# A graph layer pair on one core: two transposes given to the DMA engines, one compare given to VectorE, and a new written-out order

## The chip, the cores and the metric

The kernel runs on one core of one Trainium2 chip. A core has TensorE (PE in the profile, with PEld for its weight loads), VectorE (DVE), ScalarE (ACT), GpSimd (POOL) and SyncE (SP, which only issues DMAs here), and 16 DMA engines behind them. The metric is device microseconds of one execution. Of three timed runs of the kernel before, the median is 966.61 us (966.36 to 968.12).

## The reference

There are 128 graphs of 128 nodes with 64 features. With F = 64 and H = 192 the reference computes, for each graph b:

```
# layer 0
mask = adj > 0
h[j,k,:] = relu(x[j] @ W1a + (x[j] - x[k]) @ W1b + b1)         # 128 x 128 x 192
hm[j,:]  = sum over k of h[j,k,:] * mask[j,k]
x = layernorm(x + hm @ W2 + deg[j] * b2)
# layer 1
m   = relu(relu(x @ V1 + c1) @ V2 + c2)
msg = relu(adj @ m)
r, z, n = GRU gates of (msg, x)
x = layernorm(x + (1 - z) * n + z * x)
```

The sum over k runs only over the neighbours of j, and most nodes have few. So the kernel gathers the projected rows of the neighbours with matmuls against one-hot matrices, and does not form all 128 x 128 pairs.

## The kernel before

The 128 graphs are worked off in 32 groups of G = 4 graphs. For one group the work is a set of named parts, each a Python generator whose steps end at `yield`:

- `load`: three kinds of DMA on SP's queue (`adjT`, `xT` in two halves, `x`), lines 397, 403 and 405.
- preparation: `masks` (POOL, L415), `ranks` (a matmul with a triangular matrix gives the rank of every neighbour in its row; ACT copies it to `rankT`, L425), `degrees`, `counts`, `offsets` (first segment numbers, then `till`, four POOL compares of `iota` with a per-partition limit `off`, L466, then a matmul L469 that gives `own`, the owner of each extra segment), `turned` (four PE transposes of `rankT`, L487, and an ACT copy, L490), `owners` (four PE transposes of `own`, L495, and an ACT copy to fp32, L498), `places` (9 matmuls that need `rank` and `own`, L504 to L511), `pick0` and `pick1` (VectorE compares that make the one-hot matrices, L518, L532, L540), `values0` and `pieces` (the projections, split into three bf16 pieces).
- the gathers, the bulk: `seed0`/`seed1` (ACT writes a start value to a PSUM tile, L606), `gather0`/`gather1` (12 matmuls 64 x 192 each, L636, 24 such steps for a group), and their readers, `keep0`/`keep1` (ACT relu, L656) and `reduce`/`reduce1` (VectorE relu and add in one instruction, L666, 18 for a group). A PSUM tile is read before the next gather adds to it; there are three such tiles (pool `ps_g`).
- `base`, `together`, `joined` (ACT and POOL fold the sums), `sums0`/`sums2` (PE, L711, L718 and L723, for graphs 0, 1 and 2, 3; the second uses `ownT`).
- the tail of a group, made by `tail_parts`: `second` (L284, L288, layernorm), `turn`, `message1` to `message3`, `gates`, `update` (layernorm and the store, L743). For the last group `filler` adds matmuls without use between steps of this chain.

Small PSUM tiles of all these parts share a pool `ps_w` with two buffers.

The order is written out by hand. TIMETABLE gives each step of each part a number; group g adds g * PER to it (PER = 100000), FIRST replaces some numbers for group 0 and SETUP gives those of the constants. All steps are sorted by number and emitted in that order, and each engine then works through its own instructions in that order. So parts of four or so groups are interleaved, and the numbers set only the order and not a time. Every engine's queue, SP's too, is strictly in order: an instruction that waits holds all that stand behind it.

After the groups a branch for inputs with too many neighbours follows, which is not taken here; its test costs a small matmul and a register load at the end.

Of the kernel before, what the change touches and what calls it, by code (L numbers as in the profile page):

```python
# [8 lines left out]
F32 = mybir.dt.float32  # L9
BF16 = mybir.dt.bfloat16  # L10
I32 = mybir.dt.int32
AF = mybir.ActivationFunctionType
ALU = mybir.AluOpType
AX = mybir.AxisListType

N = 128
# [15 lines left out]
    "load": (-268618,), "masks": (-266066,), "ranks": (-232900, -232900), "degrees": (-257102, -254423),  # L32
    "turned": (-224742, -220574), "counts": (-234901,), "offsets": (-217678, -211964, -197704, -192380, -189932),
    "owners": (-35894, -35894), "places": (-179586, -177714),
    "pieces": (-221915, -212465, -212465, -212025, -212025, -210034, -207896, -206287, -204509, -201502, -201502),
    "others": (-93885, -63613), "values0": (-168677, -168312, -168312), "pick0": (-187243, -177588, -157318, -147219),
    "pick1": (-101562, -99096), "over0": (-86465, -86465), "over2": (-91716, -89070), "base0": (-71690,),
    "base1": (-115079,), "base2": (-74898,), "base3": (-66289,), "together0": (-90368, -86071, -54801),
    "sums0": (-16639, -16639, -6895), "joined0": (-42043,), "joined2": (-9054,),
    "together1": (-31159, -22707, -22707), "together2": (-54332, -29252, -26680), "sums2": (-10324, -7550, -6743),  # L40
    "together3": (-14410, -11697, -11388), "second": (1322, 1729, 6614, 12070, 12714, 14947), "turn": (17589, 19125),
    "message1": (22148, 22871), "message2": (24221, 25357), "message3": (34134, 47496),
    "gates": (52002, 52335, 59212, 59212, 60471, 61641),
    "update": (63484, 134926, 134926, 146356, 147450, 212137, 231447, 236648, 276814),
    "seed0": (-137838, -111380, -107532, -90909, -89996, -88760, -70167, -48540),
    "gather0": (-132826, -123102, -109699, -102053, -101463, -95122, -90696, -82750, -82750, -77811, -77618, -69952,
        -66122, -48012, -38905, -32104), "keep0": (-129922, -97944, -81962, -65602),
    "reduce": (-116740, -102949, -100299, -89511, -89215, -81357, -75312, -71801, -69013, -44762, -33692, -24596),
    "seed1": (-80653, -43141), "gather1": (-77673, -72671, -67801, -55447, -41338, -33923, -28108, -20295),
    "keep1": (-76545, -38998), "reduce1": (-70927, -59829, -52180, -31003, -23063, -16037),  # L50
# [3 lines left out]
SETUP = (-227883, -212853, -185033, -155144, -101231, 22249)  # L54
FIRST = {
    "load": (-236749, -176840), "masks": (-192323,), "ranks": (-160512, -153527), "degrees": (-172354, -159518),
    "turned": (-108605, -102394), "counts": (-146837,), "offsets": (-115482, -109556, -106790, -103472, -99536),
    "places": (-98687, -93949),
    "pieces": (-169807, -166786, -164278, -164278, -164278, -164278, -158634, -152826, -143767, -142875, -113691),
    "values0": (-148521, -139633, -130220), "pick0": (-141784, -133982, -133982, -103074), "pick1": (-92485, -74065),  # L60
    "over0": (-88306, -87641),
# [4 lines left out]
def adj_resnorm_kernel(  # L66
# [172 lines left out]

    def tail_parts(s, work, ps_w, n, store):


        name = s["name"]


        side = nc.vector if name == str(ng - 1) else nc.gpsimd

        def layernorm(y, tag, into):  # L250
            stats = work.tile([N, n, 6], F32, tag="st" + tag, name=f"stats{tag}_{name}")
# [640 lines left out]
```

## Time and profile before

| what | value |
|---|---|
| median of three runs | 966.61 us |
| the profiled execution's own time | 966.97 us |
| its span in the profile | 965.2 us |
| granted TensorE clock, mean | 0.980 |
| PE busy | 907.4 us, 94% |
| DVE busy | 827.3 us, 86% |
| ACT busy | 841.4 us, 87% |
| POOL busy | 840.7 us, 87% |
| distance between equal steps of two groups in the middle | 28.29 us |

Busy time of an engine is the union of its instructions; a group's row gives the number of instructions, their summed time and the mean of one, and then the idle time just before them with the engine that ended it. In a timeline row the first number is the start and the second the length, both in us.

### The profile page before, as it was taken

To read this page: it belongs to the slowest core of one execution; us is meant where nothing else is said; L and a number is where in the kernel's file an instruction comes from. 1 tells how busy PE (TensorE), PEld (TensorE's weight loads), DVE (VectorE), ACT (ScalarE), POOL (GpSimd) and SP (SyncE) were. 2 spreads that over 40 slices of the span, in tenths; PEclk is the share of its full clock that TensorE was granted. 3 is DMA by queue.
4 is the path that set the end of the run, shared out by engine and by line. 5 is a ranking of instruction groups with operands and counts; after the bars stand their busy time and mean duration, and the time that the engine had idled before them with its cause. 6 is when DMAs were issued, how large, how long until landed. Compare 5 with 4: busy or idle time off the path is not lost.

```text
span 965.2 us, 32667 instructions
## 1 busy us (share of the span) xinstructions
PE 907.4 (94%) x13333; PEld 723.1 (75%) x13335; DVE 827.3 (86%) x1586; ACT 841.4 (87%) x1762; POOL 840.7 (87%) x1233
## 2 busy tenths in 40 slices
PE   6888999999999999999999999999999999999984
PEld 3567777777877777878777787777778777777762
DVE  5687898888899888889988888988888898888962
ACT  3787899999999999999999999999999999999863
POOL 4576899999999999999999999999999999999774
PEclk6898999999999999999999999999999999999998
DMA  3000001111100111110001111011101001010000
GB/s 97 24 3 23 24 2 29 30 29 30 29 18 13 30 30 29 30 30 10 22 29 30 30 30 29 2 30 30 30 29 29 25 7 30 29 30 8 7 7 19
DMA packets 25565, 23.91 MB, mean 25 GB/s; under 512 B 4156, under 2 KB 21314, under 8 KB 25410
## 3 DMA queue, kind: packets, MB, share of 16 engines
q1 hardware_dynamic: 25410, 21.78, 7.9%
q8 instruction: 106, 1.74, 0.8%
q14 instruction: 49, 0.40, 0.1%
HBM read 17.57 MB, written 4.19 MB: 23 GB/s over the span
## 4 chain that ended last, share of the span: by engine, by line
PE 68%; ACT 14%; DVE 13%; issue 3%; POOL 1%; DMA 0%; SPq 0%; ACTq 0%; DVEq 0%; POOLq 0%
PE pv L636 32%; DVE acc L666 7%; ACT x L269 4%; PE ph L718 3%; PE pw L284 3%; PE pv L577 3%; ACT pv L606 3%; DVE pick L532 3%; ACT us L623 2%; PE pv L547 2%; PE pu L547 2%; PE ph L723 2%; PE ph L711 2%; PE pm L307 2%; PE pa L327 2%
## 5 line engine op out<-in xcount | busy, mean ns | idle before, releaser
L666 DVE SCALAR_TENSOR_TENSOR acc<-pv,acc 128x768 f32<-128x768 f32 x576 | 534.4, 952 | 102.6 <-PE pv L636 90.4
L636 PE MATMUL pv<-b,pick 64*128 64x192 bf16 x9216 | 465.9, 245 | 21.0 <-DVE acc L666 17.0
L636 PEld LDWEIGHTS <-pick 64*128 64x128 bf16 x9216 | 379.2, 95 | 92.9 <-issue 69.9
L606 ACT COPY pv<-u 128x768 f32<-128x768 f32 x256 | 206.3, 816 | 1.1 <-DVE acc L666 1.0
L656 ACT ACTIVATE acc<-pv 128x768 f32<-128x768 f32 x192 | 155.9, 812 | 17.1 <-PE pv L636 16.9
L686 POOL TENSOR_TENSOR acc<-acc 128x384 f32<-128x384 f32 x128 | 143.7, 1123 | 12.9 <-DVE acc L666 12.9
L466 POOL TENSOR_SCALAR till<-iota,off 128x128 bf16<-128x128 bf16 x128 | 100.3, 801 | 7.8 <-ACT off L458 7.8
L574 ACT CAST b<-pv 128x384 bf16<-128x384 f32 x192 | 83.0, 486 | 19.7 <-PE pv L547 10.5
L691 POOL TENSOR_TENSOR fs<-acc,nb 128x192 f32<-128x192 f32 x128 | 75.9, 593 | 21.6 <-ACT nb L678 14.1
L699 POOL TENSOR_TENSOR acc<-acc 128x384 f32<-128x384 f32 x64 | 77.8, 1216 | 7.3 <-DVE acc L666 7.2
L688 POOL TENSOR_TENSOR acc<-acc 128x192 f32<-128x192 f32 x128 | 77.9, 608 | 2.6
L518 DVE TENSOR_TENSOR pick<-rankT,ramp 128x2048 bf16<-128x2048 bf16 x64 | 77.2, 1208 | 0.7 <-POOL npad L448 0.7
L606 ACT COPY pv<-us 128x768 f32<-128x768 f32 x64 | 51.4, 803 | 26.4 <-DVE acc L666 26.4
L259 POOL TENSOR_SCALAR ve<-mv 128x4 f32<-128x4 f32 x64 | 39.5, 617 | 35.5 <-DVE mv L256 35.4
L263 POOL TENSOR_TENSOR rs<-ve,nhalf 128x4 f32<-128x4 f32 x64 | 66.8, 1043 | 0.0
L415 POOL TENSOR_SCALAR maskT<-adjT 128x512 bf16<-128x512 f32 x32 | 61.2, 1912 | 6.1 <-DMA adjT<-in_adjT_dram 6.0
L617 PE MATMUL pz<-u,own 128*128 128x192 f32 x256 | 57.7, 348 | 0.9 <-ACT own L474 0.9
L678 ACT ACTIVATE nb<-u,npad 128x192 f32<-128x192 f32 x128 | 58.5, 458 | 0.0
L532 DVE TENSOR_TENSOR pick<-pick 128x1024 bf16<-128x1024 bf16 x64 | 50.4, 787 | 0.0
L269 ACT ACTIVATE x<-y,nm,rs 128x64 f32<-128x64 f32 x128 | 45.9, 432 | 4.8 <-POOL nm L265 4.8
L269 ACT ACTIVATE o<-y,nm,rs 128x64 f32<-128x64 f32 x128 | 45.9, 446 | 2.2 <-POOL nm L265 2.2
L617 PEld LDWEIGHTS pz<-u,own 128*128 128x128 f32 x256 | 39.8, 189 | 9.3 <-ACT own L474 5.9
(148 smaller groups left out, 1635.6 us busy)
## 6 DMA issues: line engine op xcount, KB each, us to landing
adjT<-in_adjT_dram SPq DMA_DIRECT2D x32, 256.0 KB, 3.0
xT<-in_xT_dram SPq DMA_DIRECT2D x64, 64.0 KB, 2.7
x<-in_x_dram SPq DMA_DIRECT2D x32, 128.0 KB, 2.3
out_dram<-o SPq DMA_DIRECT2D x32, 128.0 KB, 1.7
wab<-in_w_dram SPq DMA_DIRECT2D x2, 96.0 KB, 2.9
bi<-in_b_ih_dram SPq DMA_DIRECT2D x1, 96.0 KB
bias<-in_b_hh_dram SPq DMA_DIRECT2D x1, 96.0 KB
wx<-in_w_hhT_dram SPq DMA_DIRECT2D x2, 48.0 KB, 2.7
```

The costliest lines, as they stand in the source:

```text
L269: nc.scalar.activation(s[into][:, i, :], y[:, i, :], AF.Identity, bias=nm[:, i : i + 1], scale=rs[:, i : i + 1])
L466: nc.gpsimd.tensor_scalar(s["till"][:, i, :], iota, off[:, i : i + 1], None, ALU.is_lt)
L532: nc.vector.tensor_tensor(v[:, q, 1], v[:, q, 1], v[:, q, 0], ALU.subtract)
L574: nc.scalar.copy(b[c][:, h::2, :], ps[h])
L606: nc.scalar.copy(v, src.to_broadcast(list(v.shape)))
L617: nc.tensor.matmul(p[:, i, :], s["own32"][:, i0 + i, :], s["u"][:, i0 + i, :], start=True, stop=True)
L636: nc.tensor.matmul(v[:, h, j, :], pick[ks], s[f"b{c}"][ks, gr, :], start=False, stop=c == 2, skip_group_check=True,)
L656: nc.scalar.activation(kept(s, t, i), view(s["pv", t, i, 0]), AF.Relu)
L666: nc.vector.scalar_tensor_tensor(out=a, in0=view(s["pv", t, i, k // CH if t == 0 else 0]), scalar=0.0, in1=a, op0=ALU.max, op1=ALU.add,)
L686: nc.gpsimd.tensor_tensor(f[:, 0], f[:, 0], f[:, 1], ALU.add)
L688: nc.gpsimd.tensor_tensor(f[:, 0, 0], f[:, 0, 0], f[:, 0, 1], ALU.add)
L699: nc.gpsimd.tensor_tensor(f[:, 0], f[:, 0], f[:, 1], ALU.add)
```

## The change

- `turned` and `owners` no longer use PE and PSUM. Each is one transposing DMA on SP's queue (128 x 512 bf16, four 128 x 128 blocks); `rank` comes straight from it, `ownT` is copied from a new bf16 tile `ownTh` (one buffer) to fp32 by ACT as before.
- `off` and its ACT copy are gone. `till` is one VectorE compare of 128 x 512 that reads the limits from PSUM, in place of four POOL compares of 128 x 128.
- The first group's `adjT` and `xT` are issued on ScalarE's queue.
- In the last group layer 1 is worked off as two pairs of graphs: parts with the ending `_a` for graphs 0 and 1, without fillers, and the usual parts for graphs 2 and 3. The dimensions that were 2 become n // 2.
- `sums` gets one more `yield`, between L718 and L723 of before.
- TIMETABLE, SETUP and FIRST are new throughout. Loads of a group stand 3.74 periods ahead of its base number where they stood 2.69 ahead, and `second` 1.02 periods ahead where it stood 0.01 behind; so the distance between the two is nearly the same.

```diff
 def loading(s):
-                nc.sync.dma_start(s["adjT"], adjT[:, gs, :])
+                q = nc.scalar if g == 0 else nc.sync
+                q.dma_start(s["adjT"], adjT[:, gs, :])
...
-                    nc.sync.dma_start(s["xT"][h * F : (h + 1) * F], xT[:, g * G + h : (g + 1) * G : 2, :])
+                    q.dma_start(s["xT"][h * F : (h + 1) * F], xT[:, g * G + h : (g + 1) * G : 2, :])
...
 def offsets():
-                off = prep.tile([N, G], F32, tag="off", name=f"off{g}")
-                nc.scalar.copy(off, p[:, 1, :])
                 s["woff"] = prep.tile([N, G], BF16, tag="woff", name=f"woff{g}")
                 nc.scalar.mul(s["woff"], p[:, 0, :], 2.0 * W1)
                 yield
                 s["till"] = prep.tile([N, G, N], BF16, tag="till", name=f"till{g}")
-                for i in range(G):
-                    nc.gpsimd.tensor_scalar(s["till"][:, i, :], iota, off[:, i : i + 1], None, ALU.is_lt)
+                nc.vector.tensor_tensor(s["till"], each(iota, G), wide(p[:, 1, :], G, N), ALU.is_lt)
                 yield
...
 def turned():
-                p = ps_w.tile([N, G, N], BF16, tag="w", name=f"pr{g}")
-                for i in range(G):
-                    nc.tensor.transpose(p[:, i, :], s["rankT"][:, i, :], ident_h)
-                yield
                 s["rank"] = prep.tile([N, G, N], BF16, tag="rank", name=f"rank{g}")
-                nc.scalar.copy(s["rank"], p)
+                nc.sync.dma_start_transpose(s["rank"], s["rankT"].rearrange("p g n -> p (g n)"))
+                yield
 def owners():
-                p = ps_w.tile([N, G, N], BF16, tag="w", name=f"pq{g}")
-                for i in range(G):
-                    nc.tensor.transpose(p[:, i, :], s["own"][:, i, :], ident_h)
+                t = prep.tile([N, G, N], BF16, tag="ownTh", name=f"ownTh{g}", bufs=1)
+                nc.sync.dma_start_transpose(t, s["own"].rearrange("p g n -> p (g n)"))
                 yield
                 s["ownT"] = prep.tile([N, G, N], F32, tag="ownT", name=f"ownT{g}")
-                nc.scalar.copy(s["ownT"], p)
+                nc.scalar.copy(s["ownT"], t)
...
-    def tail_parts(s, work, ps_w, n, store):
+    def tail_parts(g, work, ps_w, n, store, lo=0, fill=True):
...
-            if name == str(ng - 1):
+            if fill and name == str(ng - 1):
...
-            s["x1T"] = work.tile([N, 2, N], F32, tag="x1T", name=f"x1T{name}")
+            s["x1T"] = work.tile([N, n // 2, N], F32, tag="x1T", name=f"x1T{name}")
...
-            parts = {"load": loading(s), **prep_parts(s), **tail_parts(s, work, ps_w, G, storer(g))}
+            parts = {"load": loading(s), **prep_parts(s)}
+            if g < ng - 1:
+                parts.update(tail_parts(s, work, ps_w, G, storer(g)))
+            else:
+                early = tail_parts(s, work, ps_w, 2, storer(g), fill=False)
+                parts.update({f"{k}_a": v for k, v in early.items()})
+                parts.update(tail_parts(s, work, ps_w, 2, storer(g, 2), lo=2))
...
 TIMETABLE = {
-    "turned": (-224742, -220574), "counts": (-234901,), "offsets": (-217678, -211964, -197704, -192380, -189932),
-    "owners": (-35894, -35894), "places": (-179586, -177714),
+    "turned": (-272568, -171369), "counts": (-333387,), "offsets": (-310900, -305943, -303488, -292051, -285534),
+    "owners": (-153741, -131732), "places": (-270818, -268534),
...
+    "second_a": (-111100, -110015, -107069, -106567, -103378, -99663), "turn_a": (-92426, -81714),
...
+    "gates_a": (-2585, 1906, 7556, 8397, 14259, 14787),
```

## The prediction

> **What bounds the kernel now.** I read the busy shares first, then one period in the middle by its windows, then the waits, then the chain for the length of a period, and last the timeline around the removed instructions. From the page (busy time, share, instructions), from its costliest groups (summed time, mean ns, idle before), and from the same groups with shapes kept apart:
>
> ```profile
> PE 907.4 (94%) x13333; PEld 723.1 (75%) x13335; DVE 827.3 (86%) x1586; ACT 841.4 (87%) x1762; POOL 840.7 (87%) x1233
> L666 DVE SCALAR_TENSOR_TENSOR acc<-pv,acc 128x768 f32<-128x768 f32 x576 | 534.4, 952 | 102.6 <-PE pv L636 90.4
> L466 POOL TENSOR_SCALAR till<-iota,off 128x128 bf16<-128x128 bf16 x128 | 100.3, 801 | 7.8 <-ACT off L458 7.8
> L490 ACT COPY rank<-pr 128x512 bf16<-128x512 bf16 x32 | 18.7, 586 | 1.1 <-PE pr L487 1.0
> L458 ACT COPY off<-po 128x4 f32<-128x4 f32 x32 | 6.3, 198 | 0.0
> L370 POOL TENSOR_TENSOR uc<-ub,tn 128x256 f32<-128x256 f32 x31 | 35.7, 1151 | 0.0
> L370 DVE TENSOR_TENSOR uc<-ub,tn 128x256 f32<-128x256 f32 x1 | 0.4, 426 | 0.0
> ```
>
> The windows view of one period (PE, PEld, DVE, ACT, POOL busy), two entries of the chain in order of time, one period's rate apart by 29 groups, and two waits:
>
> ```profile
> 385.87:414.15 28.28, 27.68 (x418) 22.27 (x420) 25.14 (x49) 26.09 (x56) 26.56 (x39) 1.00 0.09 26
> ...
> 94.74 1.03 PE pw L284 x8
> ...
> 915.24 1.03 PE pw L284 x8
> ...
> DVE acc L666 <- PE pv L636: 90.4, 105, 4.5
> ...
> PE pv L636 <- DVE acc L666: 17.0, 40, 1.7
> ```
>
> (915.24 - 94.74) / 29 = 28.29 us for a group. In it TensorE is busy 27.68 at full clock, 98%; the other three have 1.7 to 3.1 us to spare. TensorE waits for VectorE 17.0 us in all, VectorE for TensorE 90.4, 2.8 a group. So TensorE sets the period; before 94.74 is the filling, after 915.24 the last group.
>
> **The removed transposes (L487, L495).** From the timeline of that period, and SP's part of it:
>
> ```profile
> 395.70 0.23 PEld L495 LDWEIGHTS <-own 128*128 128x128 bf16 x4 [0.35 <-DVE n L356]
> 395.71 0.40 PE L495 MATMUL pq<-ident_h,own 128*128 128x128 bf16 x4
> 396.05 0.67 PE L636 MATMUL pv<-b,pick 64*128 64x192 bf16 x12
> ...
> 398.56 0.23 PEld L487 LDWEIGHTS <-rankT 128*128 128x128 bf16 x4 [0.16 <-issue]
> 398.56 0.40 PE L487 MATMUL pr<-ident_h,rankT 128*128 128x128 bf16 x4
> 398.89 0.67 PE L636 MATMUL pv<-b,pick 64*128 64x192 bf16 x12
> ...
> 400.04 0.35 SPq L743 DMA_DIRECT2D out_dram<-o  x1
> 400.48 0.38 SPq L397 DMA_DIRECT2D adjT<-in_adjT_dram  x1
> 400.92 2.16 SPq L403 DMA_DIRECT2D xT<-in_xT_dram  x2
> 403.18 0.54 SPq L405 DMA_DIRECT2D x<-in_x_dram  x1
> ```
>
> From the start of the four transposes to the next gather is 0.34 and 0.33 us, and weight loads idled 0.35 and 0.16 before them. Without them TensorE has between 0.67 (the gaps reappear at the neighbour) and 1.18 us less a group. In the built order TensorE's waits for other engines fall from 56 to 52 a group, though `places` now waits for a DMA and `sums` is cut by one `yield`; so I take the gaps as gone: 1.18.
>
> **`till` on VectorE.** One 128x512 instruction comes to VectorE. Before has none of this form; VectorE's 128x256 fp32 add (426 ns, L370) and its 128x768 add from PSUM (952, L666) lie on both sides, and a straight line gives 0.69 us. The lower bound is a third of L540's 1028 ns for 1536 bf16, 0.34; the upper is 0.95. The operand is fp32 in PSUM, so I take 0.69. VectorE goes from 25.14 to 25.8, or from 25.5 (the busiest neighbouring period) to 26.2. POOL loses 4 x 0.80 = 3.2 and falls to 23.4, which shortens nothing in the middle: it was not the bound.
>
> **ScalarE** loses the copies of `off` (0.20) and `rank` (0.59): 26.09 to 25.3. `ownT`'s copy now reads SBUF; L606 reads SBUF and L656 PSUM at the same 128x768 for 816 and 812 ns, so I cost it at nothing, with L678 (458 ns for 192 columns from SBUF, against 488 for 384 from PSUM in L623) as a bound of +0.15. ScalarE's 2 us of spare time cover it.
>
> **The two DMA transposes.** SP does nothing for most of a period: it waits 719.8 us in 30 waits for the store's `o`. In the new order it issues, for each group, the store, the four loads, `rank` and then `ownTh` of the group before. After `o` that is 0.35 + 3.1 us of issuing, then the transpose. Each moves 128 KB, as `x` (2.3 us to landing) and the store (1.7) do; the slowest row to landing is `b2bc`, 4.8. I take 2.3, with 0.35 to 1.08 us to issue as the other DMAs. Between the store's place and `places` the new order has 9 gather steps (0.50 each, since 36 matmuls take 1.66 us and 12 take 0.67: 4.5), the sums and pieces (3.6), `offsets` (0.6), `second` (1.8), `over` (1.8), `values0` (1.2) and `turn` (0.7) on TensorE: 14.2 us. Less ScalarE's four L269 (1.4) and 3.9 of SP's issuing, 8.9 us stay for the landing: hidden. `ownTh` has some 20 us. Each SP DMA also waits for the eighth before it; with seven a group that one is a period old. The Trainium skill, page "VectorE: DVE Perf Modes", section "The three transpose paths", puts one 128x128 bf16 transpose at 390 ns on TensorE and 1309 ns by DMA, and advises TensorE where PSUM will do. By it, as an estimate, a transposing DMA would take 4 x 1.31 = 5.2 us, still inside the cover; no run here shows it yet. It speaks for the rival of the late transposes, whose time and chance are worked out below from rows.
>
> **The new order.** Spare time shrinks most on VectorE. At a period of 27.1 it must idle no more than 1.3 us (27.1 less 25.8), against 3.1 now. One stretch is against that: between the tenth and the fourteenth `gather0` step VectorE has 8 adds (7.4), the degrees (0.3), one L518 (1.2) and the four gate instructions (1.1), 10.0 us; TensorE has 9 gather steps (4.5), degrees (0.2), three messages (2.2) and gates (2.3), 9.2. Up to 0.8 us a group of TensorE can be lost there, or nothing if VectorE comes in early. Ends: -0.8 and 0; I take the middle, 0.4. The gain is then 1.18 - 0.4 = 0.78 us a group, a period of 27.5, and over 29 periods 22.6 us. Ends 0.38 x 29 = 11 and 1.18 x 29 = 34.
>
> **Head.** POOL's `till` was on the chain for 2.36 us at 25.51; VectorE does it in 0.69, a gain of 1.7. The ScalarE queue takes 0.4 us off SP. But in the new order each half of group 0's `xT` stands behind a wait for an earlier small transfer (`w2c`, `bias`), issued at 3.2 to 4.7 us and about 2.0 to landing: `xT` is issued at 5.5 to 6.9 against 6.49, so its landing gains nothing. I take 2; ends 0 and 5 (first gather now at 18.50, TensorE idle 20 us before 88).
>
> **Tail.** From the last `second` (941.30) to the end of the last L269 (962.2) one chain of latencies runs. With half the columns the last x and o scalings fall from 1.44 to 0.72 each, four VectorE steps of `update` from 0.43 to about 0.28, and group 30's statistics (0.51 + 0.28 on the chain) now stand before the gates: 2.8 us. POOL's 0.23 + 0.23 + 1.04 + 0.20 doesn't shrink, and the first pair's `gates` follow the second pair's, since both need the two `ps_w` buffers, so its `update` comes last. I take 3; ends 0 and 7 (all of the chain's instructions halved, without interference).
>
> **Sum.** 966.97 (the profiled execution: span 965.2 and 1.8 around it) - 22.6 - 2 - 3 = 939.4. The median stood 0.36 below that execution: 939. The likeliest case's own range: 966.6 - 34 - 3 - 4 = 925 to 966.6 - 11 - 0 - 0 = 956.
>
> **Rivals.**
> *VectorE becomes the bound.* If it keeps today's 2.8 us of waits for TensorE because the gathers still come in bursts, a period is 25.8 + 2.8 = 28.6, at most 26.2 + 2.8 = 29.0. At 28.8: +0.5 x 29 = 15, less 5 of the ends: 977, slower. It decides from 2.5 us of VectorE idle. For it: VectorE would be at 94% even at 27.5. Against: its waits stand at TensorE's projection and sums stretches, which the new order spreads among more gathers (`sums` cut in two). 0.13.
> *The transposes come late.* `places` stands in TensorE's queue before the gathers, so every microsecond over 8.9 to landing is lost each group. At 10.5 us: 1.6 x 29 = 46 more than forecast, 985. For it: no row shows a transposing DMA, and two a group share SP with the loads. Against: DMA engines are at 0.09 share. 0.07.
> *The gain is eaten but not more.* The period lands between 27.85 and 28.25 through waits of TensorE for adds: about 960. 0.12, of it 0.03 within 0.2% of before (0.2%, 1.9 us, is about what a measurement of this kernel can tell from no change).
> *Everything lines up.* TensorE also loses its present 0.6 us of idle a group: period 26.6 to 26.9, with the ends 920 or below. 0.05.
> *The DMA transposes are hidden but the first group isn't.* `rank` of group 0 stands on SP behind 16 setup DMAs, issued until 19.78 + 0.59 before; `places` of that group came at 30.46. Covered by 10 us; at worst some us, inside the head's end of 0.
>
> **How the numbers follow.** Forecast 0.63. Faster: 0.63 + 0.05 + 0.09 = 0.77; same 0.03; slower 0.13 + 0.07 = 0.20. The range leaves out below 922 (0.05) and above 977, the half of the VectorE case and the late transposes (0.13): 922 to 977.
>
> **What the profile after would show.** No L487 or L495 rows; VectorE's `till` near 0.69 us, 32 times; the distance of equal steps near 27.5; VectorE's idle a group 1.3 to 1.8 and its waits for TensorE near 45 us in all; TensorE's waits for L666 above 17.0; SP rows of the transposes landing well before the first `places` matmul, which waits for no DMA; the last `second` to the end 3 us shorter. The forecast is wrong if the VectorE idle stays above 2.5 us a group, if L511 or `ownT` waits for a DMA, or if the transposing DMAs lengthen other work.

## The result, and the profile after

The changed kernel takes 961.62 us (median of 12, 959.23 to 966.28) against 967.41 us before on the same chip (966.36 to 969.2): a ratio of 0.9944, 95% interval 0.993 to 0.9958. It is 0.56% faster. The prediction said 939: the sign and the range held, the size did not. The profiled execution is the longest of the twelve, 966.28 us with a span of 964.5; a second profiled execution of the same kernel, taken among the experiments, has a span of 960.0. Both are used below.

From the page of the changed kernel (first profile): busy time by engine, the chain's shares (the chain is the work that ended last, followed back from the end), and two groups, whose rows in the kernel before stand last.

```profile
PE 899.8 (93%) x13081; PEld 711.2 (74%) x13084; DVE 861.4 (89%) x1628; ACT 834.4 (87%) x1705; POOL 771.6 (80%) x1113
PE 53%; ACT 25%; DVE 16%; issue 5%; POOL 1%; ACTq 0%; DVEq 0%; POOLq 0%
L688 POOL TENSOR_TENSOR acc<-acc 128x192 f32<-128x192 f32 x128 | 130.7, 1021 | 5.1
L518 DVE TENSOR_TENSOR pick<-rankT,ramp 128x2048 bf16<-128x2048 bf16 x64 | 91.5, 1432 | 0.0
```

```profile
L688 POOL TENSOR_TENSOR acc<-acc 128x192 f32<-128x192 f32 x128 | 77.9, 608 | 2.6
L518 DVE TENSOR_TENSOR pick<-rankT,ramp 128x2048 bf16<-128x2048 bf16 x64 | 77.2, 1208 | 0.7 <-POOL npad L448 0.7
```

The 256 transposes are gone from TensorE (252 matmul records fewer in all) and POOL has lost 69 us, but VectorE has gained 34 where 32 x 0.69 = 22 were forecast. The chain's first line before was `PE 68%; ACT 14%; DVE 13%; issue 3%; POOL 1%; DMA 0%; SPq 0%; ACTq 0%; DVEq 0%; POOLq 0%`: TensorE's share of it has fallen by 15 points and ScalarE's has risen by 11.

The groups with shapes kept apart, the windows of one period in the middle (the same columns as before), and the waits:

```profile
L666 DVE SCALAR_TENSOR_TENSOR acc<-pv,acc 128x768 f32<-128x768 f32 x576 | 536.2, 949 | 62.4 <-PE pv L636 46.7 <-ACT woff L465 0.4 <-ACT pv L606 0.4
L470 DVE TENSOR_TENSOR till<-iota,po 128x512 bf16<-128x512 bf16 x32 | 21.7, 679 | 4.1 <-ACT woff L465 4.1
L498 ACT CAST ownT<-ownTh 128x512 f32<-128x512 bf16 x32 | 19.9, 622 | 0.0
```

```profile
457.83:486.33 28.50, 27.48 (x411) 21.91 (x409) 26.47 (x50) 25.92 (x54) 24.23 (x35) 1.00 0.14 35
```

```profile
DVE acc L666 <- PE pv L636: 46.7, 78, 2.2
...
PE pv L636 <- DVE acc L666: 17.0, 41, 1.3
...
PE pv L636 <- ACT acc L656: 10.3, 37, 1.0
...
PE pv L636 <- ACT pv L606: 8.3, 32, 1.3
```

A period is 28.50 us where the forecast was 27.5 and before had 28.29: the middle has become longer, not shorter. VectorE waits half as much for TensorE as before (46.7 for 90.4), as forecast; but TensorE's waits for VectorE stay at 17.0, and it waits 18.6 us for ScalarE's keeps (L656) and seeds (L606) where it had waited 2.5.

The DMA issues of the transposes (the number behind the count is the median in us from issue to landing):

```profile
rank<-rankT SPq DMA_TRANSPOSE x32, 2.7
ownTh<-own SPq DMA_TRANSPOSE x32, 2.3
```

No row of the waits names either of them: they are hidden, as forecast.

Three marks in time divide the span: the start of `second` of group 1 and of group 30, and the end. From the timeline's rows of that step's first matmul (L284 before, L290 after), in us:

| profiled execution | group 1 | group 30 | mean period | group 30 to the end | span |
|---|---|---|---|---|---|
| before | 94.67 | 915.17 | 28.29 | 50.0 | 965.2 |
| after, first | 86.95 | 913.70 | 28.51 | 50.8 | 964.5 |
| after, second | 85.74 | 912.82 | 28.52 | 47.2 | 960.0 |

By the second: head -8.9, middle +6.6, tail -2.8, in all -5.2. So the gain lies where little of it was expected, and the 22.6 us of the middle are not there at all.

### The profile page after: what moved, and what is told of

Same layout as the page of the kernel before. It is cut to its first block, busy times and chain, and to the rows that moved or that the text cites. A ratio compares the mean times of both kernels' runs of the same rounds, so it can differ in the third digit from the quotient of the medians.

```text
span 964.5 us, 32114 instructions
## 1 busy us (share of the span) xinstructions
PE 899.8 (93%) x13081; PEld 711.2 (74%) x13084; DVE 861.4 (89%) x1628; ACT 834.4 (87%) x1705; POOL 771.6 (80%) x1113
## 4 chain that ended last, share of the span: by engine, by line
PE 53%; ACT 25%; DVE 16%; issue 5%; POOL 1%; ACTq 0%; DVEq 0%; POOLq 0%
PE pv L636 25%; DVE acc L666 10%; ACT pv L606 7%; PE ph L718 4%; ACT x L275 3%; PE pw L290 3%; PE pv L547 3%; ACT acc L656 3%; ACT b L574 3%; ACT us L623 3%; PE ph L724 2%; PE pw L294 2%; DVE n L362 2%; ACT own L476 2%; PE pm L313 2%
## 5 line engine op out<-in xcount | busy, mean ns | idle before, releaser
L666 DVE SCALAR_TENSOR_TENSOR acc<-pv,acc 128x768 f32<-128x768 f32 x576 | 536.2, 949 | 62.4 <-PE pv L636 46.7
L636 PE MATMUL pv<-b,pick 64*128 64x192 bf16 x9216 | 476.8, 244 | 42.3 <-DVE acc L666 17.0
L636 PEld LDWEIGHTS <-pick 64*128 64x128 bf16 x9216 | 383.8, 95 | 130.0 <-issue 106.0
L606 ACT COPY pv<-u 128x768 f32<-128x768 f32 x256 | 204.7, 805 | 2.8 <-DVE acc L666 2.1
L656 ACT ACTIVATE acc<-pv 128x768 f32<-128x768 f32 x192 | 154.1, 803 | 14.2 <-PE pv L636 11.4
L686 POOL TENSOR_TENSOR acc<-acc 128x384 f32<-128x384 f32 x128 | 128.0, 1000 | 25.3 <-DVE acc L666 25.3
L688 POOL TENSOR_TENSOR acc<-acc 128x192 f32<-128x192 f32 x128 | 130.7, 1021 | 5.1
L518 DVE TENSOR_TENSOR pick<-rankT,ramp 128x2048 bf16<-128x2048 bf16 x64 | 91.5, 1432 | 0.0
L269 POOL TENSOR_TENSOR rs<-ve,nhalf 128x4 f32<-128x4 f32 (+1 forms) x66 | 86.1, 1305 | 0.0
L699 POOL TENSOR_TENSOR acc<-acc 128x384 f32<-128x384 f32 x64 | 78.0, 1219 | 0.5 <-DVE acc L666 0.5
L606 ACT COPY pv<-us 128x768 f32<-128x768 f32 x64 | 51.9, 811 | 24.5 <-DVE acc L666 24.5
L730 ACT COPY hmT<-ph 128x384 f32<-128x384 f32 x64 | 30.6, 478 | 36.9 <-PE ph L724 36.9
L532 DVE TENSOR_TENSOR pick<-pick 128x1024 bf16<-128x1024 bf16 x64 | 56.4, 882 | 0.0
L678 ACT ACTIVATE nb<-u,npad 128x192 f32<-128x192 f32 x128 | 53.8, 445 | 0.0
L422 POOL TENSOR_SCALAR maskT<-adjT 128x512 bf16<-128x512 f32 x32 | 48.3, 1510 | 4.4 <-DMA adjT<-in_adjT_dram 4.4
L376 POOL TENSOR_TENSOR uc<-ub,tn 128x256 f32<-128x256 f32 x31 | 51.1, 1648 | 0.0
```

The lines of the kernel that those rows point to most:

```text
L269: nc.gpsimd.tensor_tensor(rs, ve, nhalf[:, 0:n], ALU.pow)
L518: nc.vector.tensor_tensor(s[name][:, rows], s[src].rearrange("p (o g) n -> p o g n", o=1).to_broadcast([N, n, G, N]), ramp[:, first : firs ...
L606: nc.scalar.copy(v, src.to_broadcast(list(v.shape)))
L636: nc.tensor.matmul(v[:, h, j, :], pick[ks], s[f"b{c}"][ks, gr, :], start=False, stop=c == 2, skip_group_check=True,)
L656: nc.scalar.activation(kept(s, t, i), view(s["pv", t, i, 0]), AF.Relu)
L666: nc.vector.scalar_tensor_tensor(out=a, in0=view(s["pv", t, i, k // CH if t == 0 else 0]), scalar=0.0, in1=a, op0=ALU.max, op1=ALU.add,)
```

## The experiments

Marks below are from the same rows; "period" is the mean from group 1 to group 30.

### Which part does it: undoing and doing one part

**Both new operations in the old order**, `owners` issued earlier so that its DMA has time (FIRST gets its own number for it):

```diff
-    "owners": (-35894, -35894), "places": (-179586, -177714),
+    "owners": (-150000, -35894), "places": (-179586, -177714),
```

> The kernel before with its own order, tail and first transfers, but with both transposes by DMA and till on VectorE; only owners is issued earlier, so that ScalarE does not wait for it. Theory A (the new order eats the gain, the operations save what was forecast): the period falls from 28.29 to 27.2 to 27.6 us and the whole to 935 to 945 us. Theory B (VectorE, with 0.7 us more of its own and with one-hot compares that are slower beside POOL, sets the period whatever the order): the period stays at 28.2 to 28.6 and the whole at 965 to 975.

1188.8 us, ratio 1.2302 (1.2282 to 1.2323), a period of 35.62. Its waits say why:

```profile
ACT own L469 <- PE pp L466: 78.6, 30, 3.7
...
PE ph L704 <- ACT hmT L722: 61.8, 30, 2.1
...
PE pw L284 <- DVE till L463: 43.3, 30, 1.7
```

`till` now reads its limits from PSUM, and at its old place it comes late. Until then it holds one of the two `ps_w` buffers, so `second` (`pw`) waits for it once a group and `sums` (`ph`) for the other buffer. Neither theory's range is met. This run does not tell what the operations are worth; the place of one reader hides it.

**The new order with the old operations**, first both, then one at a time put back as they were before (the transposes with their PSUM tile and, in TIMETABLE and FIRST, an earlier `turned`; `till` with its copy `off`); the edits that are not the change read backwards:

```diff
-    "turned": (-272568, -171369), "counts": (-333387,),
+    "turned": (-340000, -330000), "counts": (-333387,),
...
-                nc.vector.tensor_tensor(s["till"], each(iota, G), wide(p[:, 1, :], G, N), ALU.is_lt)
+                for i in range(G):
+                    nc.gpsimd.tensor_scalar(s["till"][:, i, :], iota, off[:, i : i + 1], None, ALU.is_lt)
```

> The changed kernel with its order, pairs and first transfers, but with the transposes on TensorE (issued somewhat earlier, so that nothing waits for their copies) and till on POOL as before. Theory A: TensorE's 0.7 to 1.2 us a group come back on top of 28.5, so a period of 29.2 to 29.7 and 985 to 1000 us. Theory B: VectorE is relieved, so the period is 28.0 to 28.5 and the whole 950 to 960.

> The changed kernel with only till (and the copy of off) back on POOL and ScalarE. Theory A: VectorE's 0.6 us was hidden, period 28.4 to 28.7. Theory B: VectorE was the bound, the period falls by 0.4 to 0.7, to 27.8 to 28.1, and the whole to about 945 to 950.

> The changed kernel with only the two transposes back on TensorE and ScalarE. Theory A: TensorE is still the bound under the new order, so the period rises by 0.7 to 1.2 to 29.2 to 29.7 us (985 to 995 us in all). Theory B: TensorE is not the bound, the period stays at 28.5 to 28.7 (960 to 966).

Measured: both old operations 1055.62 us (1.0918; 1.09 to 1.0937), only `till` on POOL 1027.68 (1.062; 1.0601 to 1.0639), only the transposes on TensorE 980.3 (1.0138; 1.0121 to 1.0155; period 29.09). The first two are far above both theories, the third lies just under theory A. Two waits of the run with only `till` on POOL, which the kernel before does not have at this size:

```profile
PE pv L639 <- ACT acc L659: 54.9, 35, 1.8
...
ACT x L275 <- POOL nm L271: 40.0, 30, 1.4
```

In the new order POOL's four compares stand ahead of the layer norm's small instructions; ScalarE waits for those with its scaling `x`, and the keeps queued behind it come late for TensorE. So the new order fits the new operations, and each undone alone looks like a large gain (0.59 us a group for the transposes) that, by the next runs, exists only inside it.

**The operations alone in the old order**: the DMA transposes (with the edit of `owners` above and nothing else), then both, then `till`, these two with `till` right behind its matmul (in FIRST too):

```diff
-    "offsets": (-217678, -211964, -197704, -192380, -189932),
+    "offsets": (-217678, -211964, -211900, -192380, -189932),
```

> The kernel before with only the two transposes by DMA (owners issued earlier), its own order, till on POOL as before. Theory A (the removed transposes save TensorE 0.7 to 1.2 us a group where the old order stands): period 27.1 to 27.6, 940 to 950 us. Theory B (something else than TensorE sets the period): 28.1 to 28.4, 960 to 968.

> As the first run (new operations, old order), but till stands right behind the offsets matmul, so that the small PSUM tile whose limits it reads is free at once. Theory C (the 1186 us came from that tile: VectorE read it late, and one of the two ps_w buffers was held): 935 to 965 us, period 27.2 to 28.2. Otherwise, if the new operations themselves do not fit the old order, over 980.

> The kernel before with only till on VectorE, right behind the offsets matmul, transposes on TensorE as before. If VectorE's extra 0.6 us and the place in its queue cost nothing: 960 to 968 us. Theory B (VectorE near the bound): period 28.5 to 29, 975 to 990.

DMA transposes alone 967.89 us (1.0012; 1.0002 to 1.0021), period 28.28. Both 969.62 (1.0022; 1.001 to 1.0035), 28.37. `till` alone 971.07 (1.0047; 1.0031 to 1.0064), 28.43. The 1.2302 was the held buffer, though the second run stays above its expected 965. And the first of these is the main finding: eight matmuls a group are gone from TensorE, and the period is the same to a hundredth. The windows, waits and chain of that kernel (its L632, L652 and L662 are L636, L656 and L666 of before):

```profile
376.59:404.88 28.29, 27.19 (x411) 21.93 (x409) 25.46 (x49) 25.77 (x54) 26.33 (x39) 1.00 0.14 34
```

```profile
PE pv L632 <- ACT acc L652: 20.8, 58, 1.5
```

```profile
393.57 0.55 ACT rz L353 x2
...
394.17 0.81 ACT acc L652
...
396.02 0.51 ACT ownT L494
...
396.90 0.83 ACT acc L652
...
397.77 0.67 PE pv L632 x12
```

20.8 us over 31 groups are 0.67 us, just what the shortest view of the transposes gave them. Where TensorE had transposed, it now waits for a keep on ScalarE, whose stretch from 393.57 to 397.73 carries the chain. From TensorE's timeline, the gather behind the place of `owners`, the one behind the place of `turned`, and the next one but one, behind L543 (L547 of before):

```profile
395.03 0.67 PE L632 MATMUL pv<-b,pick 64*128 64x192 bf16 x12 [0.46 <-ACT acc L652]
...
397.77 0.67 PE L632 MATMUL pv<-b,pick 64*128 64x192 bf16 x12 [0.16 <-ACT acc L652]
...
399.04 0.67 PE L632 MATMUL pv<-b,pick 64*128 64x192 bf16 x12
```

The kernel before shows that nothing could be won there. Two rows of it, ScalarE's keep and VectorE's add beside the transposes that the prediction shows:

```profile
395.19 0.81 ACT L656 ACTIVATE acc<-pv 128x768 f32<-128x768 f32 x1
...
399.05 0.95 DVE L666 SCALAR_TENSOR_TENSOR acc<-pv,acc 128x768 f32<-128x768 f32 x1
```

The keep ends at 396.00, and the gather behind the transposes of `own` starts at 396.05; so it is in 28 of 32 groups. The add ends at 400.00, and the gather behind L547 starts at 400.08. A gather that was waiting for a tile starts about 0.04 us after the reader's end (399.04 above, after an add that ends at 398.99). So before the change the transposes stood in time in which TensorE would have waited for a reader anyway, to within 0.05 us at either place: counted from the start of `second` (377.61 before, 376.59 here), the first of these gathers starts 18.44 us in both kernels and the last 22.47 and 22.45.

### What sets the period

**The ScalarE stretch?** `ownT`'s copy moved out of it, ahead of the values' copies, where ScalarE idled 0.56 us:

```diff
-    "owners": (-150000, -35894), "places": (-179586, -177714),
+    "owners": (-150000, -68350), "places": (-179586, -177714),
```

> The kernel before with the two DMA transposes in the old order, and one step more: ScalarE's copy of ownT, 0.58 us, is issued ahead of the values' copies, where ScalarE idled 0.56 us for a matmul, and no longer among rz, the keeps and tn, where ScalarE worked without a pause from 393.55 to 404 while TensorE waited 20.8 us in all for the keeps (L652). Theory R (without the transposes that ScalarE stretch is the next thing that sets the period): those waits fall below 8 us, the period from 28.28 to between 27.6 and 27.9, the time to about 953 (948 to 958). Rival (three tiles of PSUM and their three readers give the same period wherever the copy stands): the waits move to another releaser, period 28.1 to 28.3, 963 to 968.

968.18 us (1.0009; 0.9998 to 1.002), period 28.29. TensorE's waits for the keeps went from 20.8 only to 16.9, and nothing was won. The copy stands behind the first of the two waits (0.46 us) and could shorten only the second (0.16), behind which VectorE's add sets the next gather as before. So the copy is not what holds the period; whether it would shorten if the keep at 394.17 came ahead of `rz`, behind which it is queued, was not tried.

**VectorE?** Its two subtractions left out, in the changed kernel and in the old order with DMA transposes:

```diff
-                v = s["pick0"].rearrange("p (q h c) g n -> p q h c g n", q=2, h=2)
                 for q in range(2):
-                    nc.vector.tensor_tensor(v[:, q, 1], v[:, q, 1], v[:, q, 0], ALU.subtract)
                     yield
```

> The changed kernel without the two VectorE subtractions of pick0 (L532, 0.88 us each, 1.76 a group); what is left out is the step from bins to differences, so the sums are others. If VectorE is what closes the ring in the new order (busy 26.5 of 28.5), the period falls by 1.0 to 1.8 us, to 26.7 to 27.5, and the time to 910 to 935. If TensorE or ScalarE do, it stays at 28.2 to 28.5 and the time above 953.

> The same two subtractions left out of the kernel before with the DMA transposes in the old order (what is left out is the step from bins to differences). If ScalarE's stretch sets that period, VectorE's 1.57 us a group bring at most 0.3: 27.9 to 28.3. If VectorE is in the ring there too, 27.0 to 27.5.

Periods 28.53 and 28.27, times 961.16 (0.9934; 0.9912 to 0.9955) and 966.05 (one execution). VectorE's busy time fell from 26.47 to 25.27 in a period of the changed kernel, by 1.20 and not by the 1.76 of the expectation; nothing came of it. VectorE alone isn't the bound either, in neither order.

**TensorE, the other way round.** Each transpose of the kernel before done twice:

```diff
-                for i in range(G):
+                for i in 2 * list(range(G)):
                     nc.tensor.transpose(p[:, i, :], s["rankT"][:, i, :], ident_h)
```

(and the same for `own`)

> The kernel before with each of the eight transposes done twice, so with 0.67 us or more of TensorE added a group at the places where the change takes 0.67 away. Theory T (TensorE's own work sets the period, the step of the prediction): +0.67 to +1.18 us a group, 986 to 1001. Theory Q (several paths of equal length, TensorE's one of them): the same here, though taking work from one path alone brought nothing. Theory S (these two places are never on the path that sets the period): 0 to +0.15 a group, 967 to 971.

980.23 us (1.0132; 1.0116 to 1.0147), period 28.73: +0.44 us, below the 0.67 of theories T and Q and above the 0.15 of S. The windows of a period, and one of the two places:

```profile
438.32:467.06 28.74, 28.13 (x427) 22.70 (x425) 25.48 (x49) 26.30 (x55) 26.56 (x39) 1.00 0.09 25
```

```profile
398.95 0.62 PE L495 MATMUL pq<-ident_h,own 128*128 128x128 bf16 x8
399.51 0.67 PE L636 MATMUL pv<-b,pick 64*128 64x192 bf16 x12
```

From the start of eight transposes to the next gather 0.56 us pass where four took 0.34, so the doubling adds 0.22 us here, as much at the other place, and no 0.67: TensorE's busy time grew from 27.68 to 28.13, and the period grew by all of it. Added, such work costs its full price; taken away, it brings 0.01. That speaks for Q, paths of nearly equal length: adding to one makes it the longest, shortening one leaves the others.

**The busiest engine, or the hand-overs?** The changed kernel without the subtractions and without the third piece of the gathers' operand:

```diff
-                        for c in range(3):
+                        for c in range(2):
...
-                                    start=False, stop=c == 2, skip_group_check=True,
+                                    start=False, stop=c == 1, skip_group_check=True,
```

> The changed kernel without the subtractions of pick0 and without the third piece of the gathers' operand, so eight of twelve matmuls a step: TensorE loses about 4.4 us a group of its 27.5, VectorE 1.76 (what is left out is the step to differences and the lowest bits of the gathered values). The largest engine is then ScalarE with 25.8. Theory T (the busiest engine sets the period): 26.0 to 26.4, 875 to 890 us. Theory R (a chain of hand-overs sets it: a gather of 0.5 us, its reader of 0.95, the next gather into the same tile; some ten of these a group, so it shortens by a tenth to a fifth of what TensorE loses in all): 27.2 to 27.8, 918 to 940.

930.36 us (0.9625; 0.9602 to 0.9647), period 27.41. The windows of a period and the chain's shares from its page:

```profile
440.93:468.35 27.42, 24.50 (x314) 17.99 (x312) 24.75 (x48) 25.36 (x54) 23.37 (x35) 1.00 0.14 37
```

```profile
ACT 37%; DVE 22%; issue 21%; PE 19%; DMA 1%; POOL 0%; SPq 0%; ACTq 0%; DVEq 0%; POOLq 0%
```

TensorE is busy 24.50 where it was 27.48, and every engine now idles at least 2.06 us of each period (ScalarE, the busiest, 25.36 of 27.42). Yet the period gave 1.1 of TensorE's 3.0. The theory of the busiest engine (26.0 to 26.4) falls, the range of the hand-overs (27.2 to 27.8) holds, though not by its own terms: it took a tenth to a fifth of a loss of 4.4, and more than a third of 3.0 came. In such a hand-over a gather writes a PSUM tile, a reader on ScalarE or VectorE takes it, and only then the next gather may write that tile. The changed kernel's own chain shows such a passage (start, us, what):

```profile
470.41 0.65 PE pv L636 x12
471.06 0.04 issue
471.10 0.95 DVE acc L666
472.05 0.06 DVE pick L518
472.11 1.07 issue
473.18 0.96 DVE acc L666
...
474.16 0.80 ACT pv L606
...
476.44 0.88 DVE acc L666
...
477.36 1.74 PE pv L636 x36
```

From 471.06 to 477.36 the chain is not on TensorE, though TensorE works through most of it: gather, add, an L518 that stands between two adds on VectorE, add, seed, and so on to the gather at 477.36. TensorE sat idle for only 0.04 us just before that gather, so its own path is nearly as long here too. In the old order the keep and the add shown above hold what the transposes leave; which hand-overs set 28.51 in the new order wasn't settled, and the `pick0` subtractions alone do not.

### The head

The changed kernel with the first `adjT` and `xT` on SP's queue, and the kernel before with the first steps in the new order (a shift of the whole; middle and operations as they were):

```diff
-                q = nc.scalar if g == 0 else nc.sync
+                q = nc.sync
```

```diff
-SETUP = (-227883, -212853, -185033, -155144, -101231, 22249)
+SETUP = (-282974, -224363, -188126, -178259, -122667, 22249)
...
-    "load": (-236749, -176840), "masks": (-192323,), "ranks": (-160512, -153527), "degrees": (-172354, -159518),
...
+    "load": (-184111, -169305),
+    "masks": (-176478,),
+    "ranks": (-169173, -163612),
...
+                q = nc.scalar if g == 0 else nc.sync
```

> The changed kernel with the first group's adjT and xT on SP's queue again, all else as changed. If the ScalarE queue is what made the head 7.7 us shorter, 966 to 970 us; if the new order of the head or an earlier full clock did it, within 2 us of the changed kernel, 959 to 964. The profile gives the period of the changed kernel a second time: 28.5.

> The kernel before, operations and middle order as they were, with the first adjT and xT on ScalarE's queue and the first group's own places up to pick0 (setup, load, masks, ranks, degrees, counts, pieces, values0, pick0) in the changed kernel's order, shifted as a whole. Theory H (the head's 7.7 us come from the order of the first steps and the queue alone): the last group-0 second layer (the second group's start of it) moves from 94.7 to 87 to 88.5, the period stays 28.28, time about 960. Rival (they come from the next groups' preparations being deeper, which this leaves as it was): 93 to 95, time 965 to 968.

The first: 964.54 us (0.9979; 0.9966 to 0.9993), just above the lower of the two ranges expected, group 1 at 88.68, so ScalarE's queue is worth 1.7 to 2.9 us. The second: 962.83 us (0.9954; 0.994 to 0.9968), group 1 at 89.66 where before has 94.67, period 28.29. So about five of the head's 7.7 to 8.9 us come from the first group's order and that queue alone, with nothing else of the change; the two kernels with this head further below have group 1 at 90.97 and 88.29, so this is 3.7 to 6.4. The expectation (87 to 88.5, 960) put group 1 some 1 to 3 us too early. Where the rest comes from is not shown: the deeper preparation of the groups behind was not run by itself, and `till` on VectorE, alone in the old order, has group 1 at 90.47, but at 94.51 with the DMA transposes beside it.

The clock is not the cause. The windows at 25 to 30 us of before, and of the old order with the DMA transposes (which has before's head but for those), show a granted clock of 0.50 and 1.00; the second one's group 1 starts at 93.74, only 0.9 us earlier. And the second profile of the changed kernel, at 0.50 from 10 to 20 us, starts group 1 at 85.74, ahead of the first, at 1.00 there (86.95).

```profile
25.00:30.00 5.00, 4.29 (x39) 2.82 (x38) 1.34 (x2) 4.08 (x10) 4.49 (x8) 0.50 0.25 72
```

```profile
25.00:30.00 5.00, 3.83 (x33) 2.43 (x35) 1.19 (x2) 3.64 (x9) 4.33 (x8) 1.00 0.31 61
```

### The tail

The changed kernel again, and with two more matmuls of zeros in the last group:

```diff
             filler(9)
+            if not fill:
+                for i in range(2):
+                    nc.tensor.matmul(g["spare"], ones_h, zeros, start=True, stop=True)
```

> The changed kernel once more, for a second profiled execution. In the first one the granted clock was 0.50 from 939 to 945 us, and the last group's start to the end took 27.3 us, against 23.7 in the run with the first transfers on SP's queue, whose tail is the same code at clock 1.00. Theory C (the tail's gain was there, and the clock's fall hid it in that execution): where the clock stays at 1.00, the last 23.5 to 24 us again and a span near 960.5; where it falls, 27. The period stays 28.50. Rival (the fall of the clock is the rule for this kernel): 27 us again, and the other kernel with it was the exception.

> The changed kernel with two more matmuls of zeros (0.43 us together) in the last group, right after the first pair's first layer-norm input, where TensorE idled 0.47 us ahead of the clock's fall. Theory C: the fall no longer happens, executions scatter less (within 0.4%), median 960 to 961. Rival (the fall has another cause, or the matmuls cost what they save): 961 to 966 with the same scatter.

Again: 961.84 us (0.9939; 0.9925 to 0.9952), span 960.0, group 30 to the end 47.2. With the fillers: 962.88 (0.9954; 0.9941 to 0.9968), five executions from 962.21 to 963.09. The windows of the tail, first profile of the changed kernel and then the second (PEclk is the third number from the end):

```profile
940.00:945.00 5.00, 4.09 (x18) 2.46 (x19) 1.60 (x14) 1.15 (x3) 2.67 (x7) 0.50 0.00 0
```

```profile
940.00:945.00 5.00, 4.35 (x25) 2.31 (x25) 1.60 (x14) 2.25 (x7) 4.17 (x10) 1.00 0.00 2
```

The same code ran at half clock in the one and at full clock in the other, and took 3.6 us longer from group 30 to the end. So the tail's 2.8 us are there, and hidden in the first profile. They compare two executions without the fall. Of the nine profiles with the old last group, seven show a fall of 3.4 us there, and group 30 to the end takes 51.2 to 52.7 us in them (50.0 in the profile of before, which has none); of the nine with the pairs in the new order, only the first has one. So the pairs may be worth more than 2.8 in the median. With the fillers the scatter is 0.1%, but the median is not better; whether they prevent the fall is not shown.

### Head and tail without the rest

The kernel before, operations and middle order unchanged, with the new head and the last group in pairs (LAST holds the changed kernel's numbers for `sums2` and layer 1, shifted as a whole, and `sums0` as before); then the same with the updates of the groups 29 and 30 issued earlier:

```diff
+                times = LAST[name] if g == ng - 1 and name in LAST else TIMETABLE.get(name)
+                if ng - 4 < g < ng - 1 and name == "update":
+                    times = (74259, 85343, 87067, 92000, 93000, 120014, 143040, 162482, 176748)
```

> The kernel before in operations and in its middle order (transposes on TensorE, till on POOL), with the changed kernel's first transfers and first steps (as in the run with before's middle and the new head) and its last group in two pairs. Theory N (the change gains in head and tail alone and loses in the middle, 29 x 0.21 us): period 28.29, last group's start to the end about 24 where before has 25, 961.4 - 3 = 958, against 961.6 of the changed kernel. Rival (the tail's gain hangs on the new order or on the till and transposes): 962 or more.

> The kernel before in operations and middle order with the changed kernel's head and split last group, as in the run before it, whose tail lost 10 us: there the layer norm of the last group's second pair waited on POOL behind the update of the group before (ua, ub, uc, y, 2.9 us, and two rs). Here the updates of the last groups but one are issued ahead of the last group's layer 2. Theory N (head and tail carry the change's gain): last start to the end 24 to 25.5, span 957 to 960, time about 959, at or a little under the changed kernel's 961.8. Rival (the pairs need the new order): 30 or more, time above 965.

The first took 969.63 us (1.0031; 1.002 to 1.0042), above its rival's 962: POOL did group 30's update (ua, ub, uc, y) between the steps of the last group's layer norms, and TensorE waited 5.05 us for the second pair's `x`. The second mends that: 961.53 us (0.9945; 0.9931 to 0.9958), period 28.31, group 1 at 88.29, group 30 to the end 48.4. (These marks are of its second fastest execution, 959.37.) That is the changed kernel's time (961.62 and 961.84) without its transposes, its `till` and its middle order. No kernel that was tried and leaves nothing out is clearly below both.

## Why the prediction was right and wrong

**The step that failed: "So TensorE sets the period".** It read 27.68 busy of 28.28 as a bound and VectorE's and ScalarE's 2 to 3 us as spare. The runs show hand-overs between the engines instead, in paths as long as TensorE's own: 0.49 us of TensorE's busy time taken away (27.68 to 27.19) bring 0.01 (28.28), 0.44 added cost 0.44, 3.0 taken away bring 1.1 (27.41, with all engines idling 2 us), and 1.2 us of VectorE bring nothing. The profile before had it: ScalarE's keep ends 0.05 us ahead of the gather behind the first transposes, and the prediction's own fence has TensorE wait 0.35 us for VectorE ahead of them. The chain, of which ScalarE and VectorE held 27%, was read for two time marks only.

**"So I take the gaps as gone: 1.18".** The term measured 0.01 in the old order, outside its own ends of 0.67 and 1.18: the waits came back not beside the transposes' time but in place of it, 20.2 us in all for ScalarE's keeps (20.8 for 0.6). Fewer waiting instructions in the built order were no evidence of less waiting.

**The new order's -0.4, a period of 27.5.** Measured +0.22 against before: with the same operations the old order has 28.37, the new one 28.51. The stretch that the prediction named against itself, between the tenth and fourteenth `gather0`, is where the chain leaves TensorE (471.06 to 477.36), and of the new waits those for the seeds stand there, 6.7 us in 29 groups; those for the keeps stand earlier, 7.5 us behind the start of `second` (6.9 us in 30). So the loss was looked for in the right place in part, but set against a gain that wasn't there.

**`till` on VectorE, 0.69 us:** 679 ns, right; POOL's loss shortens nothing, right. What was missed is VectorE's total, 26.47 and not 25.8: some of its compares became slower beside POOL (below). Its idle time, 2.0 us a group, is above the 1.3 to 1.8 foreseen and below the 2.5 that was to count against the forecast. Alone, the move costs 0.14 us a group (28.43).

**ScalarE:** `ownT`'s copy from SBUF took 622 ns for 577, +0.05, inside the bound of +0.15; ScalarE's busy time fell from 26.09 to 25.92, not to 25.3. "ScalarE's 2 us of spare time" was no cover: the new waits are for ScalarE.

**The DMA transposes:** landing 2.7 and 2.3 us for the forecast 2.3; a median of 1.22 and 1.21 us to issue on SP, above the bound of 1.08; hidden, right. The estimate of 5.2 us from the Trainium skill, page "VectorE: DVE Perf Modes", section "The three transpose paths", doesn't agree with the trace: four 128 x 128 blocks in one instruction landed in half of four times its figure. The advice of the Trainium skill, in the same page's section "Rules for kernel authors", TensorE where PSUM will do, is not contradicted: the DMA brought no time.

**Head -2, ends 0 and 5:** -7.7 and -8.9, outside. The sum had costed `xT`'s landing and `till`, and left out the order of the first steps, which is worth about 5 with the queue. **Tail -3, ends 0 and 7:** -2.8 at full clock, right in size; POOL's `rs`, which "doesn't shrink", fell from 1.04 to 0.75 us, and the fall of the clock was not among its risks.

**The rivals.** "The gain is eaten but not more" (about 960) gives the time, by another way: the period did not land at 27.85 to 28.25, and head and tail pay for it. "VectorE becomes the bound" has the period (28.6) and not the cause, since VectorE relieved of 1.2 us changes nothing. That the kernel became faster at all, as forecast, is luck as far as the reasoning goes: the middle, which was to bring 22.6 us, lost 6.6, and the head brought about four times what was put down for it. **The signs in the profile after:** no transposes, `till`, hidden DMAs and 46.7 us of VectorE's waits came as said; the period, and TensorE's waits for L666 above 17.0 (they stayed at 17.0; the new ones are for ScalarE), did not.

## What to carry to other kernels

A busy share of 98% was no bound here, where each instruction's result is handed to another engine and back. Before work is taken off the busiest engine, look at the instruction behind that work and at what else it waits for: in the profile before, the reader that releases it ends 0.05 us ahead of its start, so nothing could be won. Test the bound before a large change, and in the right direction: doubling the work that is to go cost its full 0.44 and would have spoken for the change, while moving it away showed 0.01 in two small edits. A written-out order and its operations belong together, so undoing one of them inside the new order overstated what it is worth (19 and 66 us above the changed kernel's 961.6 here, though in the old order each done alone loses 1 and 4 us).

## What was not expected of the hardware

VectorE's L518 compares and POOL's adds slow each other where they overlap. From the timeline of the changed kernel:

```profile
471.97 1.29 DVE L518 TENSOR_TENSOR pick<-place,ramp 128x2048 bf16<-128x2048 bf16 x1
...
472.13 1.58 POOL L688 TENSOR_TENSOR acc<-acc 128x192 f32<-128x192 f32 x1
...
475.58 0.59 POOL L688 TENSOR_TENSOR acc<-acc 128x192 f32<-128x192 f32 x1
...
480.02 1.38 DVE L518 TENSOR_TENSOR pick<-rankT,ramp 128x2048 bf16<-128x2048 bf16 x1
...
480.40 1.46 POOL L688 TENSOR_TENSOR acc<-acc 128x192 f32<-128x192 f32 x1
```

L688 takes 0.59 us where no L518 runs beside it, and that also beside VectorE's adds L666 (28 times between 100 and 900 us), and 1.46 to 1.58 in these rows beside L518; in the mean 1021 ns where it was 608. The L518 that reads `rankT` takes 1432 ns in the mean where it took 1208; the one that reads `place` was slow in the kernel before too (1278 now, 1347 before). The Trainium skill, page "GPSIMD Engine Reference", section "1. Specifications", says that GpSimd's SBUF interfaces are shared with VectorE and that VectorE instructions with two SBUF inputs contend; the trace agrees, with these numbers: L518 reads two operands from SBUF, L666 one and the other from PSUM.

TensorE's granted clock fell to 0.50 near 939 us in one execution and stayed at 1.00 in another of the same code, with no TensorE pause over 0.58 us in the 13 us ahead of it in either; the execution with the fall took 3.6 us longer from group 30 to the end. The Trainium skill, page "TensorE: Matmul & The Clock Gate", section "Part 1: The HAM clock gate (the "warmup" mystery)", calls the window in which activity is judged free-running and the slow start run-variable, and two executions of the same code differ here too. The fall after an idle window of some 3.4 us, which its table gives, is not what this trace shows: TensorE was busy for 2.29 and 2.35 us of the two stretches of 3.4 us ahead of the fall.
